# Five outer products instead of three in a 4x2x3 block scheme, early first addends out of PSUM, and one-level Strassen for two side products

## The chip, the cores and the metric

The kernel runs on one core of a Trainium2 chip. The metric is the device time of one execution in microseconds (us): the median of repeated runs, lower is better. The core has a matrix engine (PE, with weight loads shown apart as PEld), three engines for elementwise work (DVE, the vector engine; ACT, the scalar engine; POOL, GpSimd), and queues that issue transfers (SP's and ACT's hardware queues, and POOL's own, which can add to the destination while it moves). PE writes only to PSUM, eight banks of 512 float32 per partition; everything else lives in SBUF, 128 partitions wide.

## The reference

For x of 1024 x 512, a weight of 64 x 512 x 512 (embedding e, feature f, model column m), and a linear layer of 512 x 512, all float32:

```python
out_lin = x @ lin_w.T + lin_b
xv = jnp.einsum('bf,efm->bem', x, weight)
zp = jnp.einsum('bf,efm->bem', jnp.square(x), jnp.square(weight))
interaction = 0.5 * jnp.sum(jnp.square(xv) - zp, axis=1)
return out_lin + interaction
```

The large part is `xv`: a product of 1024 x 512 with 512 x 32768, of which only the sum of squares over e is kept. The sum over e of `zp` is one product of 1024 x 512 with 512 x 512, once the squares of the weight are summed over e. `out_lin` is another product of that size.

## The kernel before, in words

**Groups.** The 512 columns m are cut into 22 groups (`GROUPS`): two of 16 columns, then twenty of 24. A group is 64 times as many columns of the large product: 1024 for the first two, 1536 for the others. The host has laid the weight out so that a group is four quadrants (feature half by column half), each of 2 x 768 elements per partition (`iw` = 768; 512 in the first two groups).

**Outer level.** Each group is one 2 x 2 by 2 x 2 block product by the Strassen-Winograd scheme: seven outer products, numbered 1 to 7 and run in `ORDER` 1, 6, 5, 2, 7, 4, 3. Their left operands X1 to X7 are made once at the start from x. Their right operands (`RHS`) are weight quadrants or sums of quadrants, which POOL's adding transfers make in place (`outer_sum`). The scheme's running sums over outer products are kept in four SBUF tiles `oa` to `od`: `TARGET` names the tile that an outer product writes and `ADDEND` the one that it adds to its own result. After outer products 7 and 4, `outer_out` adds `od` to `ob` and to `oc`, two adding transfers each.

**Inner level.** An outer product is 512 x 256 by 256 x 768, and there are two ways to do it. `tree` (L630) is again 2 x 2 x 2 Strassen-Winograd: seven products of two matmuls, 384 columns each (256 in the first two groups), so 14 matmuls. `wide_tree` (L719) is a 4 x 2 x 3 scheme: 20 matmuls of 256 columns. A float32 matmul shows in the trace as two PE instructions. Before, `HK` = (1, 5, 7) are wide in the groups of 24 and the other four are narrow; in the two groups of 16 all seven are narrow. A wide left operand needs 20 blocks in place of 14; `widen` (L542) makes them once, after the group of 16 that used X last. The right-hand sums of a product (in tile `t`) are POOL's: three instructions for a narrow one (768, 384, 384 elements), seven for a wide one (768, 512, 512 and four of 256).

**Leaving PSUM.** Four pairs of banks are shared: `b1`, `b3` ("fresh") and the ring `b2_0`, `b2_1`. A wide outer product uses three pairs: two banks T, U of a fresh pair, Q and S of one b2 pair, R and V of the other. Running sums inside PSUM are started by copies from bank to bank on ACT (`copy`) and go on by accumulating matmuls. `leave` takes a finished bank out to the target: a copy on ACT where nothing is added, else an addition on DVE. Values that are needed twice are parked by ACT in the small tiles `p5` and `p53` (rings of two buffers): `pp`, `p19` and `n5` of a wide product, `p5` of a narrow one. Where such a parked value and an `ADDEND` must both be added and the product is not in `EARLY`, POOL adds one of them (both are in SBUF) and DVE the other. Where it is in `EARLY` (before: 2 alone), DVE adds the bank to the addend at once, straight out of PSUM, and adds again later; nothing is parked and POOL does nothing.

**After a sum is complete** (outer products 2, 5, 4, 3), `finish` squares it on ACT and reduces it over e on DVE into `acc`: 16 pairs of instructions of 768 elements a group. `w_squares` does the same with the weight quadrants into `w2_sum`, eight pairs a group.

**First and last stage.** At the start, 32 matmuls of 512 columns (L503) make `out_lin`; it goes to DRAM. At the end, 32 matmuls of 512 columns (L950) multiply -0.5 x squared by `w2_sum`; DVE adds the saved `out_lin` and half of `acc`, and the result leaves.

**Order.** All instructions are put into a list (`Plan`), with costs per engine, and `Plan.order` (L175) plays that list against its cost model: each engine takes its next ready operation by latest start, PE by `key`. The result is a fixed program order for each engine. `AHEAD_OF` (L37) is a table of small shifts of the due times, one per operation kind. The costs stand in `tt`, `copy`, `square`, `reduce`, `dma`, `dma_add` (L413 to L458). PE may take an operation up to `AHEAD` = 20 us before its turn. On the chip each engine executes its list strictly in that order.

Of the kernel before, what the change touches and what calls it, by code (L numbers as in the profile page):

```python
# [12 lines left out]
AF = mybir.ActivationFunctionType  # L13
# [6 lines left out]
HK = (1, 5, 7)  # L20
EARLY = (2,)
# [14 lines left out]
SPARE = -99.0  # L36
AHEAD_OF = """  # L37
0:l 1:hvhc 2:3bp 3:hvw0 4:37v 5:338 6:3g7 7:34e 8:1o 9:33e a:33f b:-d c:369 d:-2 e:28 f:1 g:-1v h:-k i:-2k
j:-o k:-5 l:-26 m:8 n:7 o:i p:2a q:d r:15 s:b t:29 u:q v:-5 w:4 x:-k z:m 10:-9 11:d 12:-5 13:g 14:w 15:-2
16:10 17:-b 18:-e 19:17 1a:f 1b:1b 1c:l 1d:-14 1e:-c 1f:-3 1g:-11 1h:m 1i:7 1j:2 1k:8 1l:6 1m:-g 1n:-2 1o:-r  # L40
1p:-h 1q:m 1r:-r 1s:a 1t:5 1u:j 1v:-f 1w:3 1x:a 1y:o 1z:-g 20:3 21:-p 22:-g 23:g 24:2tw 25:2xs 26:f 28:38f
29:314 2a:-8 2b:-26 2c:9 2d:-4 2e:-8 2f:i 2g:-l 2h:-2 2i:d 2j:z 2k:-a 2l:13 2m:l 2n:m 2o:-7d 2p:-7 2q:-1 2r:1h
2s:-h 2t:-u 2u:ao 2v:-d 2w:-c 2x:-k 2y:7 2z:d 30:13 31:s 32:1u 33:-m 34:-j 35:-14 36:-i 37:-c 38:4 39:c 3a:18
3b:b 3c:-5 3d:l 3e:8 3f:1 3g:23u 3h:k 3i:1m 3j:g 3k:d 3l:1w1 3m:f 3n:-18 3o:-c 3p:5 3q:-i 3r:-g 3s:o 3t:-2
3u:-17 3v:3 3w:-q 3x:-t 3y:m 3z:m 40:-4 41:1rk 42:-a 43:-f 44:2 45:5 46:-1b 47:-1r 48:-4j 49:-s 4a:-t 4b:-3
4c:-o 4d:1d 4e:b 4f:2 4g:-r 4h:j 4i:-i 4j:1s 4k:-4 4l:4 4m:f 4n:3 4o:-7 4p:-l 4q:1j 4r:-b 4s:a 4t:c 4u:-2 4v:2
4w:m 4x:-1a 4y:-1 4z:-5 50:2 51:-2 52:-5 53:-5 54:r 55:x 56:13 57:n 58:20 59:1vi 5a:f 5b:-2 5c:1q 5d:-d 5e:1u1
5f:8 5g:-f 5h:3 5i:-2 5j:7 5k:36 5l:17 5m:-h 5n:-7 5o:10 5p:15 5q:i 5r:-w 5s:g 5t:f 5u:c 5v:-s 5w:1 5x:j 5y:6
5z:4d 60:e 61:13 62:d 63:-p 64:k 65:-b 66:17 67:-g 68:-k 69:-m 6a:1g 6b:x 6c:a 6d:-5 6e:5 6f:-7 6g:1e 6h:-4
6i:z 6j:-h 6k:-3h 6l:-22 6m:n 6n:-1n 6o:r 6p:y 6q:a 6r:10 6t:m 6u:-9 6v:-2 6w:2n 6x:-18 6y:-1h 6z:1 70:m  # L50
71:-1e 72:-k 73:-4 74:-3 75:-d 76:9 78:-o 79:-3 7a:-t 7b:-k 7c:-7 7d:-s 7e:b 7f:-9 7g:-1i 7h:-13 7i:19 7j:j
7k:1h 7l:-24 7m:c 7n:-2 7o:5 7p:-3 7q:q 7r:r 7s:q 7t:b 7u:1a 7v:v 7w:q 7x:-4 7y:-1p 7z:10 80:19 81:-o 82:m
83:c 84:-u 85:1 86:-1 87:-2 88:-4 89:-4 8a:-5 8b:-11 8c:3 8d:c 8e:-r 8f:x 8g:-w 8h:-u 8i:-5 8j:-1p 8k:-3
8l:-1e 8m:y 8n:o 8o:1f 8p:-1 8q:5 8r:-2 8s:1xv 8t:j 8u:7 8v:-7 8w:-f 8x:-u 8y:f 8z:1 90:e 91:6 92:-h 93:18
94:r 95:n 97:-1a 98:-c 99:-p 9a:-e 9b:8 9d:-11 9e:-3 9f:e 9g:-n 9h:-a 9j:-16 9k:-f 9l:-2 9m:h 9n:3 9o:f 9p:-5
9q:-2b 9r:v 9s:-18 9t:o 9u:o 9v:232 9w:8 9x:c 9y:-n 9z:d a0:-7 a1:-a a2:5 a3:-h a4:u a5:i a6:-d2 a7:8 a8:-n
a9:8 aa:-do ab:1a ac:i ad:-12 ae:11 af:2 ag:s ah:-n ai:-9 aj:-9 ak:3 al:l am:-fj an:-5 ao:2sx ap:d aq:13 ar:-4
as:2 at:t au:-9 av:-y aw:-l ax:-2 ay:9 az:v b0:-3 b1:-8 b2:l b3:-13 b4:g b5:-b b6:-1g b7:7 b8:-15 b9:-1 ba:-f
bc:-o bd:-b be:j bf:e bg:s bh:-1i bi:-1q bj:-1g bk:n bl:g bm:4 bn:a bo:-g bp:g bq:1 br:8 bs:-c bt:-1r bu:1e
bv:-1p bw:z bx:d by:m bz:-1f c0:-p c1:-5 c2:2 c3:q c4:-1j c5:-8 c6:j c7:e c8:-f c9:-b ca:5 cb:f cc:-k cd:1c  # L60
ce:-1n cf:-3 cg:-5 ch:-s ci:-m cj:-9 ck:-k cl:-7 cm:r cn:-a co:a cp:-n cq:-q cr:-10 cs:-w ct:b cu:-a cv:-10
cw:1g cx:-12 cy:j cz:-v d0:-14 d1:1b d2:-g d3:-g d4:8 d5:8 d6:-16 d7:n d8:j d9:-r da:-4 db:-13 dc:1d dd:-15
de:-9 df:16 dg:19 dh:d di:a dj:z dk:-a dl:-9 dm:-1w dn:-w do:-4 dp:p dq:b dr:-1w ds:2x dt:-b du:-e dv:-4 dw:3
dx:-t dy:g dz:8 e0:d e1:-5 e2:-g e3:-u e4:w e5:-r e6:j e7:4 e8:o e9:e ea:9 eb:a ec:-f ed:-16 ee:-l ef:k eg:-d
eh:-1g ei:i ej:-4 ek:-o el:-u em:5 en:-1f eo:-4 ep:5 er:7 es:s et:-1p eu:-9 ev:-b ew:o ex:i ey:-j ez:c f0:-14
f1:-u f2:-11 f3:5 f4:-l f5:c f6:-q f7:5 f8:k f9:-1 fa:-1e fb:1 fc:-1f fe:-j ff:-1 fg:5 fh:t fi:-q fj:-g fk:-8
fl:4 fm:-1o fn:10 fo:b fp:-3 fq:-13 fr:r fs:2 ft:-19 fu:1b fv:-t fw:-5 fx:-14 fy:-5 fz:-k g0:-6 g1:-6 g2:-2
g3:-1w g4:1o g6:-e g7:a g8:q g9:-d ga:-5 gb:8 gc:-h gd:9 ge:-5 gf:-7 gg:a gh:6 gi:-h gj:2 gk:-11 gl:-6 gm:4
gn:e go:1v gp:-14 gq:s gr:6 gs:-v gt:3 gu:3 gv:d gw:-6 gx:1q gy:-2 gz:-19 h0:-1m h1:-1h h2:-h h3:-5 h4:-g
h5:-14 h6:-2 h7:z h8:-j h9:f ha:-b hb:-6 hc:10 hd:-14 he:9 hf:e hg:-6 hh:-n hi:-a hj:y hk:-2 hl:-8 hn:6 ho:-t  # L70
hp:-g hq:-2 hr:-14 hs:c ht:4 hu:1 hv:a hw:-15 hx:-l hy:i hz:-d i0:-8 i1:-8 i2:-8 i3:11 i4:-7 i5:-13 i6:1h i7:b
i8:2 i9:7 ia:-8 ib:a ic:6 id:-m ie:2 if:4 ig:6 ih:-o ii:-a ij:-8 ik:n il:c im:u in:x io:-6 ip:a iq:-g ir:s
is:g it:l iu:-m iv:-1l iw:-2 ix:16 iy:-1o iz:-q j0:-y j1:-a j2:u j3:q j4:z j5:-1t j6:3 j8:-h j9:-c ja:12
# [947 lines left out]
```

## Time and profile before

| | |
|---|---|
| median of 3 runs | 1416.3 us (1412.21 to 1417.54) |
| the profiled execution | 1415.96 us |
| its span, first to last instruction | 1414.2 us |
| DVE busy | 1100.0 us (78%) x1461 |
| ACT busy | 806.0 us (57%) x1293 |
| POOL busy | 1173.7 us (83%) x1117 |
| granted PE clock, mean | 0.997 of full speed |

In the rows below, a line of a group of instructions gives the line of the code, the engine, output and inputs, the shape and the count, then the busy time in us and the mean duration in ns, then the idle time before them and what ended it. A line of the chain of waits gives its start in us, its length, and what ran. A line of the timeline gives start, length, engine, line, operation and, in brackets, the idle time before it and what released it. A line of the windows gives a stretch and, for each engine, its busy time with the number of instructions, then the PE clock, the share of the transfer engines and GB/s.

### The profile page before, as it was taken

The numbers are of one execution on the slowest core, as the hardware profiler recorded it, in microseconds if no ns is written. First come the engines' busy times: TensorE is split into PE (matmuls) and PEld (weight loads), VectorE is DVE, ScalarE is ACT, GpSimd is POOL, SyncE is SP. The second block draws the span as 40 slices with busy tenths as digits, with TensorE's granted clock in tenths as the row PEclk, the third lists the DMA queues.
The fourth block names the chain that finished last, engine by engine and source line by source line (L and its number), as shares of the span: only waits on it lengthen the run. The fifth ranks groups of instructions, "written<-read, shape, count | busy, mean of one in ns | idle before, by whom it ended". The sixth has DMA issues, their size and how long they took to land.

```text
span 1414.2 us, 16647 instructions
## 1 busy us (share of the span) xinstructions
PE 1396.6 (99%) x5160; PEld 971.5 (69%) x5160; DVE 1100.0 (78%) x1461; ACT 806.0 (57%) x1293; POOL 1173.7 (83%) x1117
## 2 busy tenths in 40 slices
PE   8999989999999999999999999999999999999998
PEld 3887757767776766767676676777677677767663
DVE  2678678878878786887879688787968878796895
ACT  1456465656757465665656566565746556574642
POOL 5999978897979798797979879897987989788870
PEclk9999999999999999999999999999999999999999
DMA  8589596777949676795968678596958859694773
GB/s 260 164 192 227 135 202 153 165 188 161 228 120 228 160 178 171 167 223 117 230 159 192 160 180 208 131 222 146 216 143 195 197 132 221 135 238 109 163 193 112
DMA packets 92599, 251.76 MB, mean 178 GB/s; under 512 B 29472, under 2 KB 30496, under 8 KB 92512
## 3 DMA queue, kind: packets, MB, share of 16 engines
q0 software_dynamic: 26448, 134.49, 49.6%
q1 hardware_dynamic: 65488, 115.17, 24.0%
q8 instruction: 42, 0.69, 0.2%
q10 hardware_dynamic: 576, 1.05, 0.2%
q14 instruction: 45, 0.37, 0.1%
HBM read 127.04 MB, written 6.19 MB: 94 GB/s over the span
## 4 chain that ended last, share of the span: by engine, by line
PE 90%; POOL 4%; DMA 4%; DVE 1%; issue 1%; ACT 0%; SPq 0%; POOLq 0%; DVEq 0%; ACTq 0%
PE b L464 51%; PE b_r L464 18%; PE b_l L464 17%; POOL t L421 2%; PE b_r L950 1%; PE b_l L950 1%; DMA oc<-od 1%; DMA T<-T1a 1%; DMA oa<-xT 1%; PE b_l L503 1%; PE b_r L503 1%; DMA w<-weight 1%; POOL X L421 1%; DMA X<-xT 0%; POOL ob L456 0%
## 5 line engine op out<-in xcount | busy, mean ns | idle before, releaser
L464 PE MATMUL b<-t,X 128*128 128x384 f32 (+1 forms) x1504 | 518.5, 474 | 1.9 <-DVE ob L421 1.1
L464 PEld LDWEIGHTS b<-t,X 128*128 128x128 f32 x1504 | 276.1, 190 | 168.4 <-DVE oa L421 18.8
L421 POOL TENSOR_TENSOR t<-t,w 128x256 f32<-128x256 f32 (+1 forms) x200 | 232.6, 1287 | 9.0 <-PE b L464 5.7
L421 POOL TENSOR_TENSOR t<-w 128x768 f32<-128x768 f32 (+1 forms) x88 | 163.0, 1860 | 88.1 <-PE b_l L464 70.5
L438 ACT ACTIVATE oa<-oa 128x768 f32<-128x768 f32 (+1 forms) x176 | 142.8, 822 | 134.5 <-DVE oa L421 132.4
L464 PE MATMUL b<-w,X 128*128 128x384 f32 (+1 forms) x576 | 193.9, 469 | 0.1
L464 PE MATMUL b_l<-t,X 128*128 128x256 f32 x720 | 189.6, 381 | 3.9 <-ACT b_l L431 3.9
L464 PE MATMUL b_r<-t,X 128*128 128x256 f32 x600 | 167.9, 383 | 0.4 <-DVE ob L421 0.3
L447 DVE TENSOR_REDUCE acc<-oa 128x12 f32<-128x768 f32 (+1 forms) x176 | 161.6, 920 | 3.7 <-ACT oa L438 3.7
L447 DVE TENSOR_REDUCE w_sum<-wsq 128x12 f32<-128x768 f32 (+1 forms) x176 | 161.5, 920 | 1.1 <-ACT wsq L438 1.0
L464 PEld LDWEIGHTS b_l<-t,X 128*128 128x128 f32 x720 | 137.2, 191 | 32.2 <-ACT b_l L431 4.5
L464 PEld LDWEIGHTS b<-w,X 128*128 128x128 f32 x576 | 109.1, 190 | 56.5 <-ACT p L431 2.1
L464 PEld LDWEIGHTS b_r<-t,X 128*128 128x128 f32 x600 | 113.9, 191 | 47.7 <-issue 5.0
L438 ACT ACTIVATE wsq<-w 128x768 f32<-128x768 f32 (+1 forms) x132 | 107.3, 821 | 38.8 <-DVE w_sum L447 16.9
L421 DVE TENSOR_TENSOR oa<-b,oa 128x768 f32<-128x768 f32 (+1 forms) x88 | 82.0, 932 | 59.6 <-PE b L464 55.7
L421 POOL TENSOR_TENSOR t<-w,t 128x384 f32<-128x384 f32 (+1 forms) x96 | 107.7, 1122 | 2.4
L431 ACT COPY b<-b 128x768 f32<-128x768 f32 (+1 forms) x94 | 71.2, 757 | 60.3 <-PE b L464 58.0
L464 PE MATMUL b_r<-w,X 128*128 128x256 f32 x400 | 99.8, 380 | 0.0
L464 PE MATMUL b<-T,X 128*128 128x384 f32 (+1 forms) x264 | 91.3, 477 | 0.6 <-DMA T<-T1a 0.6
L421 DVE TENSOR_TENSOR oa<-b,oc 128x768 f32<-128x768 f32 (+1 forms) x66 | 61.2, 930 | 34.7 <-PE b L464 32.9
L464 PEld LDWEIGHTS b_r<-w,X 128*128 128x128 f32 x400 | 76.3, 191 | 14.3
L421 POOL TENSOR_TENSOR oc<-ob,p 128x512 f32<-128x512 f32 (+1 forms) x80 | 82.3, 1105 | 3.6 <-ACT p L431 2.0
(143 smaller groups left out, 2618.1 us busy)
## 6 DMA issues: line engine op xcount, KB each, us to landing
w<-weight SPq DMA_DIRECT2D x120, 384.0 KB, 6.0
ob<-od POOLq DMA_DIRECT2D x40, 768.0 KB, 7.9
oc<-od POOLq DMA_DIRECT2D x40, 768.0 KB, 9.5
T<-weight SPq DMA_DIRECT2D x40, 384.0 KB, 4.0
w<-T POOLq DMA_DIRECT2D x20, 768.0 KB, 6.5
T1a<-weight SPq DMA_DIRECT2D x20, 384.0 KB, 3.3
w22a<-weight SPq DMA_DIRECT2D x20, 384.0 KB, 8.8
T1a<-weight POOLq DMA_DIRECT2D x10, 768.0 KB, 11.9
```

Source lines behind the costliest of these rows:

```text
L421: return f(o.ap, a.ap, b.ap)
L431: return nc.scalar.copy(o.ap, i.ap)
L438: lambda _: nc.scalar.activation(o.ap, i.ap, AF.Square), i.atoms, o.atoms)
L447: nc.vector.tensor_reduce(o, x, axis=AX.X, op=ALU.add)
L464: nc.tensor.matmul(a.ap, b.ap, w.ap, start=start, stop=True, skip_group_check=True)
L503: nc.tensor.matmul(o[j].ap, x.ap[:, ts((g * 2 + j) % (NB // 2), P)], w.ap, start=(k == 0), stop=(k == NK - 1),)
L950: nc.tensor.matmul(z.ap, view(xe[h, k // KH])[:, k % KH, ts((g * 2 + j) % (NB // 2), P)], reg("w2_sum", k * M, M).ap, start=(k == 0), stop ...
```

## The change

It makes outer products 6 and 2 wide as well (five wide, two narrow in the groups of 24), puts 3, 4, 6, 7 beside 2 into `EARLY`, cuts the two parking rings to one buffer each, and does `out_lin` and the product of the squares by one level of Strassen-Winograd (seven products `big` of eight 256-column matmuls, 56 in all). PE gets four matmuls on zeros at the start (`WARM`). At the end the squares of x are made on ACT, and the whole result is assembled by quadrants. The planner's costs for ACT's and the transfers' operations and the table `AHEAD_OF` are new, so the fixed orders of all engines are new too.

```diff
-HK = (1, 5, 7)
-EARLY = (2,)
+HK = (1, 5, 6, 2, 7)
+EARLY = (2, 3, 4, 6, 7)
...
+HALF = 0.5 ** 0.5
+WARM = 4
+P5S = 1
+P53S = 1
...
-    p5_ring = ring([make(f"p5_{k}", WIDE) for k in range(2)])
+    p5_ring = ring([make(f"p5_{k}", WIDE) for k in range(P5S)])
...
-        plan.add({ACT: 0.19 + 0.00083 * o.size}, emit, i.atoms, o.atoms,
+        plan.add({ACT: 0.06 + 0.00083 * o.size}, emit, i.atoms, o.atoms,
...
-    def dma(o, i, reads, writes, cost=2.4, land=1.5, queue=nc.sync):
-        plan.add({SP: cost}, lambda _: queue.dma_start(o, i), reads, writes, land=land)
+    def dma(o, i, reads, writes, moves=1.3, land=1.8, queue=nc.sync):
+        plan.add({SP: 0.4}, lambda _: queue.dma_start(o, i), reads, writes, land=land, queue=moves)
...
-        plan.add({POOL: 1.0}, emit, reads + writes, writes, land=2.0, queue=3.1 * rows / 1024)
+        plan.add({POOL: 0.7}, emit, reads + writes, writes, land=1.8, queue=2.5 * rows / 1024)
...
+    C = M // 2
+    lw_in(0, 0, nc.scalar)
+    x_load(0, 0, nc.sync, 2)
+    lw_in(1, 0, nc.scalar)
+    x_load(0, 1, nc.sync)
+    lw_in(0, 1, nc.scalar)
+    lw_in(1, 1, nc.scalar)
+    x_load(1, 1, nc.sync)
+    x_load(1, 0, nc.sync)
...
+    plan.add({DVE: 0.8}, lambda _: nc.vector.memset(zero.ap, 0.0), (), zero.atoms)
+    for n in range(WARM):
...
+    tt(two(lsum[1]), lw(0, 1, (M, KH)), lw(0, 0, (M, KH)), only=DVE)
+    tt(two(lsum[2]), lw(1, 1, (M, KH)), two(lsum[1]), only=DVE)
+    tt(two(lsum[4]), lw(1, 0, (M, KH)), two(lsum[2]), only=DVE)
+    tt(two(lsum[7]), lw(0, 1, (M, KH)), lw(1, 1, (M, KH)), only=DVE)
...
-    tt(x_block(5), x_in(1, 1), x_in(1, 0), True)
+    tt(x_block(5), x_in(1, 1), x_in(1, 0), True, DVE)
     minus_both(x_block(6), x_block(5), x_in(0, 0))
-    tt(x_block(7), x_in(0, 0), x_in(1, 0), True)
+    tt(x_block(7), x_in(0, 0), x_in(1, 0), True, DVE)
...
+    def outer_products(xs, ws, base_key, ready, leave):
+
+        u2, u3, m4, m5 = "b2_0", "b1", "b3", "b2_1"
+        big("b1", xs[1], ws[1], True, base_key)
+        copy(pair(u2), pair("b1"))
+        big("b1", xs[2], ws[2], False, base_key + 1)
+        leave(0, 0, "b1")
+        big(m4, xs[4], ws[4], True, base_key + 2)
+        ready(0, m4)
+        big(m5, xs[5], ws[5], True, base_key + 3)
+        ready(1, m5)
+        big(u2, xs[6], ws[6], False, base_key + 4)
+        copy(pair(u3), pair(u2))
+        big(u3, xs[7], ws[7], False, base_key + 5)
+        leave(1, 0, u3)
+        leave(1, 1, u3)
+        big(u2, xs[3], ws[3], False, base_key + 6, ((0, 0, 2), (1, 0, 2), (0, 2, 4), (1, 2, 4)))
+        leave(0, 1, u2)
...
-    for (h, q), x in xe.items():
-        dma(view(x), x_src[:, ts(q, KH), ts(h, H)], (), x.atoms)
-        plan.add(
-            {DVE: 1.24},
...
+    for (h, q), x in x2.items():
+        dma(x.ap.rearrange("p (a m) -> p a m", a=KH), x_src[:, ts(q, KH), ts(h, H)], (), x.atoms)
+        plan.add({ACT: 0.10 + 0.00083 * x.size},
+                 lambda _, x=x: nc.scalar.activation(x.ap, x.ap, AF.Square, scale=HALF),
+                 x.atoms, x.atoms)
...
+    def leave(h, c, b):
+        r = rest[h, c]
+        n = 1 if (h, c) != (0, 1) else 2
+        for k in range(n):
+            o = Reg(r.tile, r.off + k * 2 * N // n, 2 * N // n)
+            tt(o, o, reg(b, k * 2 * N // n, 2 * N // n), c == 0)
+            dma(out_dst[:, 4 * h + k * 4 // n:4 * h + (k + 1) * 4 // n, ts(c, C)],
+                o.ap.rearrange("p (a m) -> p a m", m=C), o.atoms, ())
+
+    outer_products(xs, ws, 1e6, ready, leave)
```

More of the change, by code (lines that the diff above doesn't have):

```diff
@@ new lines, in pair @@
+    def pair(name):
+        return reg(name, 0, 2 * N)
+    zero = reg("t", 0, P + N)
+    plan.add({DVE: 0.8}, lambda _: nc.vector.memset(zero.ap, 0.0), (), zero.atoms)
+    for n in range(WARM):
+        z, o = reg("t", 0, P), bank(f"b2_{n // 2}", n % 2)
+        zw = reg("t", P, N)
+        plan.add({PE: 1.8 * mm_cost(N)},
+                 lambda _, z=z, o=o, zw=zw: nc.tensor.matmul(o.ap, z.ap, zw.ap, start=True, stop=True),
+                 zero.atoms, o.atoms, key=-2000 + n, banks=o.banks(True))
@@ L519, in x_block, with lw_sum @@
+    def lw_sum(i):
+        return lambda k: Reg(lsum[i].tile, lsum[i].off + k * C, C)
     def x_block(i):
@@ new lines @@
+    other = last + 1
+    rooms = []
+    for name in (w(other, "w22"), w(other, "T1"), "w11", "X1", "X6", w(last, "T1"), "X5", "X2",
+                 "w12", "X7", "T2", "w21", "X4"):
+        rooms += [reg(name, k * 2 * N, 2 * N) for k in range(buf[name].size // (2 * N))]
+    spare = [w(other, "w22"), w(other, "T1"), "w11", w(last, "T1")]
+    spare = iter([reg(n, 2 * N, N) for n in spare])
+    rooms = iter(rooms)
+    x2 = {(h, q): next(rooms) for h, q in ((0, 0), (0, 1), (1, 1), (1, 0))}
```

390 lines of the change are left out of this document (220 added, 170 removed).

## The prediction

> **What bounds the kernel now.** First the page: how busy PE is, and whose work lies on the chain that ended last.
>
> ```profile
> PE 1396.6 (99%) x5160; PEld 971.5 (69%) x5160; DVE 1100.0 (78%) x1461; ACT 806.0 (57%) x1293; POOL 1173.7 (83%) x1117
> ...
> PE 90%; POOL 4%; DMA 4%; DVE 1%; issue 1%; ACT 0%; SPq 0%; POOLq 0%; DVEq 0%; ACTq 0%
> ```
>
> PE is busy without a break, and nine tenths of the chain is PE. A busy PE need not be at its pace, so next comes the chain in the middle of the run, for the pace and the period.
>
> ```profile
> 608.46 1.73 PE b_l L464 x8
> ...
> 614.50 15.51 PE b L464 x48
> ...
> 739.29 15.51 PE b L464 x48
> ```
>
> The pattern comes back after 739.29 - 614.50 = 124.79 us, two groups: **62.40 us a group**. A matmul is two instructions. At 384 columns one takes 15.51 / 24 = 0.646 us, at 256 columns 1.73 / 4 = 0.4325 us. A group has 4 x 14 = 56 of the first and 3 x 20 = 60 of the second: 36.2 + 25.95 = 62.1 us. So waits cost 0.3 us a group, and only PE work can be won there. Then the windows, for the other engines in a steady group, at a bad place and at the end.
>
> ```profile
> 177.60:240.00 62.40, 58.49 (x213) 41.42 (x212) 46.25 (x62) 34.23 (x56) 46.71 (x45) 0.95 0.73 164
> ...
> 302.40:364.80 62.40, 62.40 (x234) 43.46 (x233) 50.15 (x67) 37.57 (x61) 52.38 (x50) 1.00 0.79 184
> ...
> 155.00:177.60 22.60, 22.46 (x83) 15.30 (x82) 15.47 (x22) 10.89 (x17) 22.30 (x24) 1.00 0.71 180
> ...
> 1360.00:1381.00 21.00, 20.80 (x71) 13.11 (x71) 19.58 (x22) 7.94 (x12) 15.14 (x12) 1.00 0.90 219
> ```
>
> The columns are PE, PEld, DVE, ACT, POOL. In the steady group DVE has 12.2 us free and POOL 10.0. Before 178 us POOL is full; near the end DVE is. One stretch lost PE time and clock; the timeline shows why.
>
> ```profile
> 191.34 0.84 ACT L438 ACTIVATE wsq<-w 128x768 f32<-128x768 f32 x1 [5.35 <-DMA w<-weight]
> 192.09 0.58 ACT L431 COPY b_l<-b_r 128x512 f32<-128x512 f32 x1
> 192.72 1.22 PE L464 MATMUL b_l<-t,X 128*128 128x256 f32 x2 [3.91 <-ACT b_l L431]
> ...
> 198.00 1.25 PE L464 MATMUL b_l<-w,X 128*128 128x256 f32 x5
> ```
>
> A square at the head of ACT's list waited for a late weight load; the copy behind it was what PE needed. PE stood 3.91 us, and then its next 12 instructions took 198.00 - 192.72 = 5.28 us in place of 12 x 0.216 = 2.6: together 6.6 us, once.
>
> **PE's part of the change.** Products 6 and 2 go from 14 matmuls of 384 to 20 of 256: per product 14 x 0.646 = 9.04 us becomes 20 x 0.4325 = 8.65. Two per group: the need falls from 62.1 to 28 x 0.646 + 100 x 0.4325 = 61.3, **0.8 us a group, 16 us over twenty groups**. The groups of 16 columns stay narrow.
>
> **What the other engines must now do per group.** POOL first, by its groups of instructions.
>
> ```profile
> L421 POOL TENSOR_TENSOR t<-w 128x768 f32<-128x768 f32 x80 | 152.1, 1908 | 88.0 <-PE b_l L464 70.5 <-DMA w<-T 10.2 <-issue 4.7
> L421 POOL TENSOR_TENSOR t<-t,w 128x512 f32<-128x512 f32 x80 | 126.2, 1578 | 8.2 <-PE b L464 5.7
> L421 POOL TENSOR_TENSOR t<-t,w 128x256 f32<-128x256 f32 x120 | 106.4, 1094 | 0.8
> L421 POOL TENSOR_TENSOR t<-w,t 128x384 f32<-128x384 f32 x80 | 93.4, 1168 | 2.2
> L421 POOL TENSOR_TENSOR oc<-ob,p 128x512 f32<-128x512 f32 x40 | 56.1, 1410 | 0.8
> L421 POOL TENSOR_TENSOR oa<-oa,oc 128x768 f32<-128x768 f32 x20 | 47.5, 2375 | 0.1
> L421 POOL TENSOR_TENSOR ob<-p,ob 128x768 f32<-128x768 f32 x20 | 39.3, 1966 | 2.9 <-DVE p L421 2.9
> L421 POOL TENSOR_TENSOR ob<-ob,oa 128x768 f32<-128x768 f32 x20 | 36.6, 1828 | 4.5 <-ACT b_l L431 4.5
> L421 POOL TENSOR_TENSOR oc<-ob,p 128x256 f32<-128x256 f32 x40 | 32.0, 801 | 2.8 <-ACT p L431 2.0
> L421 POOL TENSOR_TENSOR X<-X 128x256 f32<-128x256 f32 x43 | 37.0, 884 | 13.6 <-ACT X L431 8.4 <-DVE X L527 4.6
> L421 POOL TENSOR_TENSOR X<-X 128x128 f32<-128x128 f32 x21 | 12.6, 701 | 0.0
> ```
>
> Right-hand sums: a narrow product needs 1.9 + 2 x 1.17 = 4.2 us, a wide one 1.9 + 2 x 1.58 + 4 x 1.09 = 9.4. Two more wide ones add 10.4. `EARLY` takes away POOL's additions for 4, 3, 6 and 7: (47.5 + 39.3 + 36.6 + 56.1 + 32.0) / 20 = 10.6. POOL stays at 52 of 61 us. I cost this at nothing: the sums run a product ahead of PE, under its matmuls; without that cover each wide product would begin some 2 us late, on its first sum.
>
> ACT exchanges five copies of 768 elements, one of 512 and one of 256 for eight of 512 and two of 256: 4608 elements both ways, in three more instructions. Its 37.57 us become 38 to 39, nothing on the path.
>
> DVE is where the work goes. Here are its durations and its spacing when work is queued.
>
> ```profile
> L421 DVE TENSOR_TENSOR oa<-b,oa 128x768 f32<-128x768 f32 x80 | 76.5, 956 | 51.8 <-PE b L464 50.8
> L447 DVE TENSOR_REDUCE acc<-oc 128x12 f32<-128x768 f32 x80 | 73.8, 943 | 0.0
> L421 DVE TENSOR_TENSOR oa<-b_l,p 128x512 f32<-128x512 f32 x40 | 25.9, 686 | 3.6 <-PE b_l L464 2.9
> ...
> 648.61 1.80 DVE L447 TENSOR_REDUCE acc<-oc 128x12 f32<-128x768 f32 x2
> ...
> 672.19 1.29 DVE L421 TENSOR_TENSOR oc<-oc,b_l 128x512 f32<-128x512 f32 x2
> ...
> 674.68 0.42 DVE L421 TENSOR_TENSOR oc<-oc,b_r 128x256 f32<-128x256 f32 x1 [0.51 <-ACT p L431]
> 675.02 0.41 DVE L421 TENSOR_TENSOR oc<-ob,b_r 128x256 f32<-128x256 f32 x1
> ```
>
> Queued instructions overlap: 768 elements every 1.80 - 0.94 = 0.86 us, 512 every 1.29 - 0.69 = 0.60, 256 every 0.34. From the code a group before has 24 reductions and 21 additions of 768, 8 of 512, 13 of 256: 45 x 0.86 + 8 x 0.60 + 13 x 0.34 = 47.9 us, and the window shows 50.15 busy. An early wide product has 5 of 512 and 10 of 256, 6.4 us; it replaces 4.3 (narrow 6), 5.2 (narrow 2) and 4.1 (wide 7). Early 4 and 3 have one more of 768 each. After: 36 of 768, 19 of 512, 38 of 256 = **55.3 us of 61.3, 90%**. With full durations (0.95, 0.69, 0.42) it would be 63.4, more than PE needs; with the busy share of before (50.15 of 53.8) 59.1. I take 55 to 59: DVE fits, with little room.
>
> What that costs PE: a narrow early product must have its first bank added out by DVE (0.96) before the product after next writes that bank (1.29 us later), so a DVE in the middle of a reduction holds PE. Two such products a group, up to 0.6 each; none, if the order keeps DVE free there. I take waits of 0.8 us a group in place of 0.3: period 61.3 + 0.8 = 62.1 would win 0.3, and without any growth 61.6 wins 0.8. The wide products, whose banks are reused only three products (1.3 us) or more after each copy, make me go between, **61.85: 0.55 x 20 = 11 us** won. Bounds: 63.4 (a loss of 20 us) to 61.3 (a win of 22).
>
> The single parking buffer: `p19` of a wide product is last read after its 16th matmul and written again after the next one's 4th, 8 x 0.43 = 3.5 us later. Nothing, unless DVE is over 3 us late.
>
> **Sums ahead of time.** `ob` now gets its first addend out of PSUM at product 3's first bank, not its fourth: 3 x 1.29 = 3.9 us earlier. It waits for the second adding transfer.
>
> ```profile
> 679.62 1.17 POOL L456 DMA_DIRECT2D ob<-od  x1
> ...
> 689.11 0.95 DVE L421 TENSOR_TENSOR ob<-b,ob 128x768 f32<-128x768 f32 x1
> ...
> DMA to landing us min/median/max: 6.6/8.4/9.5
> ```
>
> It lands at 679.62 + 8.4 = 688.0; the first reader moves from 689.1 to 685.2. It can be issued when product 7 has read `ob`, which now ends with DVE at about 676: 676 + 1 + 8.4 = 685.4. Even, within 1 us. If it is late, DVE's list stands behind that addition, reductions and other banks' additions with it, and PE for the banks; PE has products 1 and 6 to put in between. Cost 0 in the forecast, up to 1 us a group as a bound.
>
> **The start.** Lines of the timeline, the last two of the chain of waits:
>
> ```profile
> 5.50 2.05 PE L503 MATMUL b_l<-ob,oa 128*128 128x512 f32 x2 [5.50 <-DMA oa<-xT]
> ...
> 9.31 1.04 ACT L431 COPY X<-oa 128x1024 f32<-128x1024 f32 x1
> ...
> 10.52 1.02 PE L503 MATMUL b_r<-ob,oa 128*128 128x512 f32 x2
> ...
> 35.73 1.03 PE L464 MATMUL b<-t,X 128*128 128x256 f32 x4
> ...
> 1381.32 3.43 PE b_l L950 x8
> ...
> 1410.11 0.69 DVE X L421
> ```
>
> `out_lin` took 35.73 - 5.50 = 30.2 us for 64 instructions that need 64 x 0.429 = 27.5; the first ones ran at half pace. After: 56 x 0.4325 = 24.2 us. The zeros, 8 instructions, can start near 1.7 us, once DVE has written them; if six are slow and take 5 us, as 5.50 to 10.52 shows, and two take 0.43 each, they end about 7.6 with the data there; one bank copy (1024 elements, 1.0 us and two hand-overs, 1.3) has nothing beside it. 7.6 + 24.2 + 1.3 = 33.1: **2.5 us** won. Bounds: 0 (both copies and a late sum of x open) to 6 (data at 5.5, nothing open).
>
> The Trainium skill ("TensorE: Matmul & The Clock Gate", Part 1: The HAM clock gate) says that PE starts at half clock and gets the full one after about 3.4 us of activity, and loses it after an idle window of that length. The slow instructions at 5.5 us and after the 3.91 us wait agree; the zeros take that cost off the real work, by this rule as by the rows.
>
> Two more `widen` are some 5 x 0.88 + 7 x 0.7 = 9.3 us of POOL each, 18.6. Against that, `EARLY` saves six additions of 512 (two thirds of 2.06 us each, the mean of the three rows of 768: 8.2), and two sums of 1024 go to DVE (2.5 each, from the row of 768). That is 5 us more where POOL is full, due in the third group, where the 6.6 us were lost. The new order may keep that wait out, as its costs now put loads and adding transfers into one queue. I take half: **3 us** won; bounds -5 to 6.6.
>
> The Trainium skill ("GPSIMD Engine Reference", 1. Specifications) says that POOL shares SBUF interfaces with DVE and contends with DVE instructions that have two SBUF inputs. Here that speaks against the sums of x and of the linear weight that go to DVE (some 5 us of DVE by its spacing), and for `EARLY`; no row here separates it. By it the start would win 0 rather than 3.
>
> **The end.** PE needs 28.8 us from 1381.32 to its last instruction; 24.2 + 1.3 for one bank copy makes 25.5, less 2 to 3 us. But DVE is full there (19.58 of 21), gets 7.4 us more in the last group, less the squares of x that go to ACT, and now PE waits for its additions: banks are used twice. I take **1.5**; bounds -4 to 3.
>
> **The sum.** 11 + 2.5 + 3 + 1.5 = 18 us off the profiled execution's 1415.96, with the 1.8 us outside its span unchanged: **1398**. The median of the runs, 1416.3, stands 0.3 above that execution, too little to correct for.
>
> **Rivals.**
> 1. *DVE becomes the bound.* For: 90% by spacing, 63.4 by durations. Against: its idle time before was mostly waiting for PE. It decides once DVE's need passes 61.9 us a group. At 63.2 the twenty groups lose 0.8 x 20 = 16, the start and the end win 4 to 5: **1427**. Chance 0.09.
> 2. *Waits eat the gain.* The early reader of `ob` and the narrow early banks each hold PE 0.3 us more, period 62.3: 2 us won in the groups, 2.5 at the start: **1411**. For: transfers of up to 9.5 us. Chance 0.14.
> 3. *Everything fits.* Period 61.45, the one stall gone: 19 + 6.6 + 2.5 + 1.5 = 29.6 off, **1386**. For: PE waited only 0.3 us a group before. Chance 0.20.
>
> The forecast (1392 to 1408) has 0.57. A change under 0.5% (7 us) can't be told from none here: faster 0.77 (forecast and 3), same 0.14 (2), slower 0.09 (1). The range 1386 to 1413 leaves out 1 and half of 3, some 19 in 100.
>
> **What would show it.** The period between equal patterns in the chain: 61.6 to 62.1 if right. DVE's busy time in a steady group: 57 to 60. POOL near 50. Trees starting near 33 us, and near 190 us PE waits of half the 3.91 us or less. A period over 62.4 with PE waiting for DVE's `oa`, `ob` or `oc` lines would make the prediction wrong by rival 1; waits ended by `ob<-od`, by rival 2.

## The result, and where the time went

The changed kernel takes **1456.9 us** (median of 4 runs, 1450.5 to 1459.1) against 1416.3 for the kernel before (1412.2 to 1417.5): a ratio of 1.028, 95% interval 1.025 to 1.032. It is slower, where 1398 and a win of 18 us were forecast, and outside the range of 1386 to 1413. The profiled execution took 1455.98 us, with a span of 1454.2.

The page of the changed kernel: busy time by engine, and the shares of the chain that ended last.

```profile
PE 1410.9 (97%) x5744; PEld 1069.0 (74%) x5744; DVE 1252.9 (86%) x2012; ACT 808.1 (56%) x1355; POOL 1124.9 (77%) x1137
...
PE 64%; DMA 15%; DVE 8%; ACT 5%; issue 4%; POOL 4%; ACTq 0%; DVEq 0%; POOLq 0%
```

PE was 90% of the chain and is 64%: in a third of the time the chain now runs through other work. The tree of product 3 starts with a matmul of the tile w22a in every even group, so its line in the timeline is a mark for measuring. Here it is in groups 4 and 20 (counted from 0), and PE's last matmuls, first of the kernel before:

```profile
308.58 0.49 PE L464 MATMUL b<-w22a,X 128*128 128x384 f32 x1
...
1307.28 0.49 PE L464 MATMUL b<-w22a,X 128*128 128x384 f32 x1
...
1408.19 1.88 PE L950 MATMUL b_r<-w_sum,X 128*128 128x512 f32 x4
```

and of the changed kernel:

```profile
323.62 0.49 PE L487 MATMUL b<-w22a,X 128*128 128x384 f32 x1
...
1344.08 0.49 PE L487 MATMUL b<-w22a,X 128*128 128x384 f32 x1
...
1448.98 1.13 PE L544 MATMUL b<-w_sum,X 128*128 128x256 f32 x4 [0.78 <-DVE X L444]
```

The sixteen groups between the marks took 998.70 / 16 = 62.42 us each before and 1020.46 / 16 = **63.78 us** after. The 40.0 us between the ends of the last matmuls (1410.07 and 1450.11) split at the marks: 15.0 up to group 4, 21.8 in the sixteen groups, 3.2 behind group 20. The prediction had all three falling.

The load on the engines came out as forecast. The windows of the changed kernel (PE, PEld, DVE, ACT, POOL, then the granted clock, the DMA share and GB/s):

```profile
120.00:240.00 120.00, 107.25 (x436) 81.58 (x435) 92.72 (x156) 63.75 (x116) 94.48 (x102) 0.96 0.65 154
...
302.40:364.80 62.40, 61.50 (x250) 46.20 (x249) 55.08 (x91) 36.81 (x63) 47.57 (x47) 1.00 0.76 179
```

In the steady stretch of 62.4 us DVE is busy 55 us, ACT 37, POOL 48. PE lost the time in waits. Adding up, over the trace, by how much each matmul instruction starts later than 0.216 us (256 columns), 0.323 (384) or 0.429 (512) behind the one before it gives 87 us lost in the changed kernel and 24 before. The need of PE by these spacings fell by 19 us (22.5 less the 3.4 for the matmuls on zeros), its first instruction starts 3.9 us earlier, and the losses grew by 63: together the 40 us. (The expectations below put the two losses at 86 and 27.)

**One wait, taken apart.** The timeline of the changed kernel in product 6, PE, ACT and DVE:

```profile
664.96 0.57 ACT L454 COPY b_l<-b_l 128x512 f32<-128x512 f32 x1
665.07 0.41 DVE L444 TENSOR_TENSOR ob<-oa,b_r 128x256 f32<-128x256 f32 x1
665.52 0.37 ACT L454 COPY p<-b_r 128x256 f32<-128x256 f32 x1
665.59 0.70 PE L487 MATMUL b_l<-T,X 128*128 128x256 f32 x2
665.92 0.42 DVE L444 TENSOR_TENSOR ob<-oa,b_r 128x256 f32<-128x256 f32 x1 [0.44 <-ACT p L454]
666.40 0.70 PE L487 MATMUL b_r<-T,X 128*128 128x256 f32 x2
666.93 1.46 PE L487 MATMUL b_l<-T,X 128*128 128x256 f32 x6
```

Both DVE instructions are first addends: `ob` gets `oa` plus a sum that stands in the right half of a bank. ACT's copy parks the same sum as `p19`. None of the three needs another's result, all only read the bank; yet the second addition stands idle for 0.44 us and starts 0.03 after the copy ends (665.89). DVE's line names the copy as what ended its wait. (The copy itself starts 0.04 us after the first addition, but ACT was busy with the copy before it until then, so that start proves nothing.) PE's next write to that bank (product 14) was due at 666.12, 0.53 us after the pair at 665.59, which had waited too, and starts at 666.40, 0.06 after the second addition. The two instructions then take 0.53 us to the next line, not 0.43: this wait cost PE 0.10 more behind it. So, in this program, reads of one PSUM bank by ACT and by DVE are taken in turn, by semaphore. No line of kernel.py asks for it: its function `follow` ties reads of a bank to writes alone, so these semaphores come in when the program is built. No run leaves them out. The Trainium skill ("PSUM — Partial Sum Buffer", PSUM bank collisions raise a hardware error) says that two engines must be kept apart on a bank by a semaphore, reads against reads included; the trace agrees, with 0.03 to 0.04 us from one read to the next. The prediction passed that rule by.

The same turn-taking was there before the change, and at the place shown it cost PE nothing. The kernel before, product 5:

```profile
344.46 1.45 PE L464 MATMUL b<-t,X 128*128 128x384 f32 x4
...
345.10 0.37 ACT L431 COPY p<-b_r 128x256 f32<-128x256 f32 x1 [0.49 <-DVE od L421]
...
346.18 0.59 PE L464 MATMUL b_r<-t,X 128*128 128x256 f32 x2
```

and the same place after:

```profile
678.76 1.03 PE L487 MATMUL b_l<-t,X 128*128 128x256 f32 x4
...
679.62 1.34 PE L487 MATMUL b_r<-t,X 128*128 128x256 f32 x4
...
679.83 0.37 ACT L454 COPY p<-b_r 128x256 f32<-128x256 f32 x1 [0.49 <-DVE od L444]
```

The copy waits 0.49 us for DVE in both. Before, matmuls of a narrow product stood between the wide one's (the 384-column line), and PE came to the bank at 346.18, 0.7 us after the copy. After, products 1, 6, 5, 2 and 7 are all wide and follow each other, PE comes at once, and four instructions take 1.34 us in place of 1.03. Such waits between 300 and 1200 us are not much longer than before: 90 to 100 instructions of ACT and DVE waited 41 to 44 us for the other's read before, 100 to 120 waited 48 to 50 us after, by how one counts. What changed is above all that PE stands behind them. In the views of waits (us in total, times, longest) the first line is of the kernel before, the other two of the changed one:

```profile
PEld b L464 <- DVE oa L421: 20.4, 60, 1.2
...
PEld b L487 <- DVE oa L444: 22.8, 53, 2.2
PEld b_r L487 <- ACT p L454: 19.0, 37, 1.2
```

PE's weight loads wait for DVE's additions into `oa` about as before; their waits for the parked copies (`p`) at the wide products' banks are new. Added up over all such lines, those behind additions into `oa`, `ob` and `oc` grew from 32 to 50 us and those behind ACT from 9 to 47.

**The other cause** is DMA. From the page of the kernel before, KB and median us to landing:

```profile
ob<-od POOLq DMA_DIRECT2D x40, 768.0 KB, 7.9
oc<-od POOLq DMA_DIRECT2D x40, 768.0 KB, 9.5
...
w22a<-weight SPq DMA_DIRECT2D x20, 384.0 KB, 8.8
```

and of the changed kernel:

```profile
ob<-od POOLq DMA_DIRECT2D x40, 768.0 KB, 9.5
oc<-od POOLq DMA_DIRECT2D x40, 768.0 KB, 14.6
T<-weight SPq DMA_DIRECT2D x40, 384.0 KB, 3.6
...
w22a<-weight SPq DMA_DIRECT2D x20, 384.0 KB, 11.8
```

The adding transfers land later, and a load beside them takes three times as long as one alone (11.8 against 3.6 us: between 130 and 1300 us an adding transfer was under way beside every load of `w22a`, and beside 5 of 36 loads of `T`). Where the transfers of `outer_out` are left out (run no_outer_out, below), the same load needs 4.4 us:

```profile
w22a<-weight SPq DMA_DIRECT2D x20, 384.0 KB, 4.4
```

How late transfers reach PE, in the timeline of ACT and PE of the changed kernel:

```profile
661.80 0.84 ACT L461 ACTIVATE oc<-oc 128x768 f32<-128x768 f32 x1 [1.26 <-DMA oc<-od]
662.55 0.37 ACT L453 ACTIVATE oa<-b_r 128x256 f32<-128x256 f32 x1
662.82 0.59 ACT L454 COPY b_r<-b_l 128x512 f32<-128x512 f32 x1
663.33 0.38 ACT L454 COPY p<-b_r 128x256 f32<-128x256 f32 x1
...
663.76 1.99 PE L487 MATMUL b_r<-t,X 128*128 128x256 f32 x8 [0.72 <-ACT p L454]
```

A square at the head of ACT's list waits for `oc<-od`; the copies behind it are what PE needs. The one-off stall of the prediction is the same thing, larger:

```profile
187.98 0.84 ACT L461 ACTIVATE wsq<-w 128x768 f32<-128x768 f32 x1 [8.56 <-DMA w<-weight]
...
195.56 0.79 ACT L454 COPY b<-b 128x768 f32<-128x768 f32 x1
...
196.50 2.90 PE L487 MATMUL b<-t,X 128*128 128x384 f32 x4 [8.26 <-ACT b L454]
```

PE stands 8.26 us (3.91 before) and then runs at half pace: four instructions of 384 columns take 2.69 us to the next, not 1.29.

### The profile page after: what moved, and what is told of

The parts are those of the page before. It is cut to its first block, busy times and chain, and to the rows that moved or that the text cites. A ratio compares the mean times of both kernels' runs of the same rounds, so it can differ in the third digit from the quotient of the medians.

```text
span 1454.2 us, 18499 instructions
## 1 busy us (share of the span) xinstructions
PE 1410.9 (97%) x5744; PEld 1069.0 (74%) x5744; DVE 1252.9 (86%) x2012; ACT 808.1 (56%) x1355; POOL 1124.9 (77%) x1137
## 4 chain that ended last, share of the span: by engine, by line
PE 64%; DMA 15%; DVE 8%; ACT 5%; issue 4%; POOL 4%; ACTq 0%; DVEq 0%; POOLq 0%
PE b_r L487 24%; PE b_l L487 20%; PE b L487 17%; DMA oc<-od 6%; DMA ob<-od 5%; POOL t L444 2%; PE b L544 2%; DVE ob L444 2%; DVE oa L444 2%; DMA w<-weight 2%; DMA w<-T 2%; ACT oc L461 1%; DVE acc L470 1%; ACT p L454 1%; DVE w_sum L470 1%
## 5 line engine op out<-in xcount | busy, mean ns | idle before, releaser
L444 POOL TENSOR_TENSOR t<-t,w 128x512 f32<-128x512 f32 x300 | 316.6, 1112 | 76.7 <-PE b L487 67.0
L487 PE MATMUL b<-t,X 128*128 128x384 f32 (+1 forms) x864 | 287.7, 465 | 16.4 <-ACT b L454 10.2
L487 PE MATMUL b_l<-t,X 128*128 128x256 f32 x1200 | 303.3, 380 | 0.0
L487 PE MATMUL b_r<-t,X 128*128 128x256 f32 x1000 | 277.2, 387 | 8.8 <-ACT p L454 3.7
L487 PEld LDWEIGHTS b_l<-t,X 128*128 128x128 f32 x1200 | 226.8, 190 | 35.5 <-DVE ob L444 1.9
L487 PEld LDWEIGHTS b<-t,X 128*128 128x128 f32 x864 | 160.2, 191 | 110.1 <-POOL t L444 15.2
L461 ACT ACTIVATE wsq<-w 128x768 f32<-128x768 f32 (+1 forms) x132 | 107.6, 822 | 53.1 <-DMA w<-weight 37.5
L487 PE MATMUL b_l<-w,X 128*128 128x256 f32 x480 | 115.4, 379 | 0.0
L487 PE MATMUL b<-w,X 128*128 128x384 f32 (+1 forms) x336 | 110.3, 458 | 1.8 <-DMA w<-T 1.5
L444 POOL TENSOR_TENSOR t<-t,T 128x256 f32<-128x256 f32 (+1 forms) x100 | 96.5, 968 | 12.7 <-PE b_l L487 7.0
L487 PEld LDWEIGHTS b_l<-w,X 128*128 128x128 f32 x480 | 90.9, 190 | 12.9 <-ACT b_l L454 0.5
## 6 DMA issues: line engine op xcount, KB each, us to landing
oc<-od POOLq DMA_DIRECT2D x40, 768.0 KB, 14.6
w22a<-weight SPq DMA_DIRECT2D x20, 384.0 KB, 11.8
```

Source lines behind the costliest of these rows:

```text
L444: return f(o.ap, a.ap, b.ap)
L461: lambda _: nc.scalar.activation(o.ap, i.ap, AF.Square), i.atoms, o.atoms)
L487: nc.tensor.matmul(a.ap, b.ap, w.ap, start=start, stop=True, skip_group_check=True)
```

## The experiments

The theories. **D**: DVE's load (rival 1). **H**: hand-overs between engines last longer than the planner counts. **B**: shared banks, as above. **T**: late transfers. The edits keep the planner's list of each engine unless they say so. The runs that leave something out were run once each, and the changed kernel's own four runs lie 8.6 us apart, so a few us of difference in time say little; the period is the better measure, though each kernel has one trace and how far its period varies was not measured. The mark of group 4 holds the one stall near 190 us, which is 8.26 us in the changed kernel's trace, 9.2 in half_reduce, 9.4 in first_sbuf, 5.7 in half_squares, 3.1 in parked_sbuf and under 1 in act_first: several us of that column go with it, whatever was edited. The marks are the ones used above.

| run | time, us | mark of group 4 | us a group | behind group 20 |
|---|---|---|---|---|
| before | 1416.3 | 308.6 | 62.42 | 102.8 |
| changed | 1456.9 | 323.6 | 63.78 | 106.0 |
| half_reduce | 1449.2 | 322.2 | 63.51 | 104.9 |
| half_squares | 1444.7 | 318.9 | 63.38 | 105.8 |
| no_outer_out | 1427.9 | 307.7 | 63.18 | 103.5 |
| act_first | 1463.9 | 317.4 | 64.62 | 106.8 |
| parked_sbuf | 1445.3 | 317.1 | 63.11 | 112.6 |
| first_sbuf | 1444.5 | 319.8 | 63.34 | 105.5 |
| all_three | 1409.2 | 304.6 | 61.95 | 107.6 |
| after_retuned | 1429.6 | 311.6 | 62.57 | 110.4 |
| after_slack | 1424.7 | 312.3 | 62.39 | 107.6 |
| before_retuned | 1417.8 | 305.6 | 62.57 | 106.1 |
| before_slack | 1415.7 | 306.1 | 62.49 | 105.3 |
| three_wide_slack | 1430.6 | 315.9 | 63.19 | 100.9 |
| squares_only | 1412.5 | 307.3 | 62.04 | 108.8 |

**half_reduce: less work for DVE.**

```diff
                 x = x.rearrange("p (m e) -> p m e", e=E)
+            x = x[:, :, :E // 2] if len(x.shape) == 3 else x[:, :, :, :E // 2]
```

> The changed kernel in its own order of instructions, with every reduction of products with e reading only the first 32 of the 64 values it sums (so acc is computed from half of them). Nothing moves on any engine; only DVE's 24 reductions a group become shorter, by about 0.4 us each, some 10 us of DVE a group. If DVE's load is what PE waits for (theory D: 55 of 63 us a group, banks and parked copies come free late behind the queue of reductions), PE's lost time in a steady group falls from 2-3 us to under 0.7 and the period between equal patterns to 61.8 or less, the time to 1415-1425. If it is the hand-overs from ACT and DVE to PE's weight loads, each some 0.1 us longer than the order leaves room for (theory H), the reductions only stand beside them: period 62.8 or more, time 1440 or more. In between: the two share it.

1449.2 us and 63.51 us a group, with DVE's busy time in a steady window down from 55.1 to 48.4 us. D asked for 61.8 or less; 0.27 us a group is what came back. D falls as the main cause.

**half_squares: less work for ACT.**

```diff
-        square(r, r)
+        square(r, r, True)     # reads and writes only the first half of each tile's columns
```

> The changed kernel in its own order, with the squares that are made for the second half of the output on ACT covering only the first half of each tile's columns. ACT has some 6 us a group less to do, nothing moves. If ACT's copies come late because they stand in its queue behind squares, the period falls by 0.5 us a group or more and the time to 1445 or less. By theory D (DVE's load) and by theory H (length of a hand-over, not a queue) the period stays within 0.3 of the 63.2-63.9 measured, the time at 1448-1458.

1444.7 us and 63.38, 0.40 a group: the time is what "ACT's queue" asked for, the period lies between its 0.5 and the 0.3 of the others, and 4.7 us are in the mark of group 4, of which the smaller stall is 2.6. ACT's list may matter where copies stand behind squares; the main cause it is not.

**no_outer_out: no adding transfers into memory.**

```diff
             dma_add(x.ap, y.ap, 2 * iw, y.atoms, x.atoms)
+            plan.ops[-1].emit = None
```

> The changed kernel in its own order, without the adding transfers that write the outer sums to memory (the output lacks the sums of the main loop). The tiles oa, ob and oc are then free at once for their next writers. Theory T (transfers that land late hold DVE's first addition into ob and oc and, through the shared queue, the weight loads): the waits of DVE on ob<-od go, the period falls by 0.5-1 us, the stall near 190 us (about 8 us of PE waiting and 3 us at half clock) is gone; time 1425-1440. By theories D and H only the stall near 190 us can go (at most 12 us), the period stays at 63 or more: 1443-1457.

1427.9 us. The stall near 190 us is gone, and the mark of group 4 comes 15.9 us earlier, ahead of the kernel before: most of the early loss is T's. The period falls by 0.60, and 63.18 is still 0.76 above before, so T is not the whole of the steady loss.

At this point the traces showed the turn-taking described above, waits that no dependence in the plan explains. From here on B is tested, with the help of a **replay**: the five lists, each in order, with durations, spacings and hand-overs taken from the two traces, the turn-taking, and transfers fitted to their landing times. It is a calculation, and no run shows its terms by themselves (among them 0.2 us for a matmul that waited, where the pair above shows 0.10).

**act_first: the same lists, woven together otherwise.**

```diff
-    for op, engine in plan.order():
+    for op, engine in act_first(plan.order()):
+    # act_first: the five lists merged by planned start, ACT's counted 1 us earlier
```

> The changed kernel with the same list of instructions in the same order on every engine; only the order in which the lists are woven together when they are issued to the program is another: an ACT instruction is put ahead of other engines' instructions that the plan starts up to 1 us earlier. Nothing is left out. Theory B (a read of a PSUM bank by ACT and one by DVE of the same bank are kept apart by a semaphore, in the order of issue, though neither needs the other's result): the waits change sides, DVE's additions out of PSUM now stand behind ACT's copies of the same bank, and as DVE is the fuller engine the time changes by several us; in-order replay of the lists with the durations measured in the changed kernel's trace says 12 us more, so 1462-1475. Theory D (DVE's load) and theory H (length of a hand-over) see the same lists and the same true dependences and expect the time within 4 us of the changed kernel's 1457.

1463.9 us, and a period of 64.62: 0.84 us a group more with not an instruction moved on any engine. D has no way to see that; B had it within its range. (The early part came out 6 us better, so the sum is +7.) And the waits did change sides. The first line is of the changed kernel's view of waits, the second of this run's:

```profile
ACT p L454 <- DVE od L444: 9.3, 19, 0.5
...
DVE od L444 <- ACT p L454: 15.7, 20, 2.5
```

These are the same places in both, product 5's copy into `p` and the addition into `od` that reads the same bank, in 19 groups. Whichever is issued first goes first and the other waits. H could see a change only if hand-overs had grown longer; for ACT's copies behind PE they are the same (0.04 us where the copy waits for one semaphore, 0.09 in the median for two, in both traces).

**parked_sbuf: the parked copies leave the banks.**

```diff
-        copy(p19, h("U", 1))
+        copy(p19, h("U", 1), instead=reg(f"X{i}", 0, V))
...
-            copy(n5, h("S", 1))
+            copy(n5, h("S", 1), instead=reg(f"X{i}", 0, V))
```

> The changed kernel in its own order, with ACT's 140 copies of 256 columns into the parking buffers (p19 and n5 of the wide products) reading a tile of SBUF in place of the PSUM bank, so that these sums are wrong; ACT's time is the same. PE no longer waits for these copies and no copy shares a bank with a DVE addition. Theory B: the period falls from 63.2-63.9 to about 62.7-63.0, the time by some 15 us to 1438-1446, as these copies carry 19 of the 50 us that ACT and DVE wait for each other's reads between 300 and 1200 us. Theory D: the period stays (DVE does what it did), 1450 or more. Theory H: the two hand-overs to PE per wide product that went give back at most 0.1 us each, 5 products x 0.1 x 20 = up to 10 us, 1447 or more.

1445.3 us, B's time, at 63.11 a group, a little over B's 62.7 to 63.0; ACT and DVE do as much as ever. By the time alone H's 1447 or more is not ruled out, one run against another. Behind group 20 it loses 6.6 us, which stays unexplained.

**first_sbuf: the first addends leave the banks.**

```diff
-                tt(f(o, *at), f(a, *at), h(b, half), sub)
+                tt(f(o, *at), f(a, *at), h(b, half), sub, instead=f(a, *at))
```

> The changed kernel in its own order, with the first addends of the wide products 6, 2 and 7 (DVE's additions that now read a PSUM bank ahead of time) taken from SBUF alone: the addend is copied by a DVE instruction of the same number of elements and the bank is not read, so that these sums lack a term. DVE's list and load stay; these instructions neither wait for ACT's reads of the bank nor hold ACT's reads or PE's next write. Theory B with the first addends as its main carrier: period 62.9-63.3, time 1436-1446 (replay: 14 us less). If the missing narrow products between the wide ones are the whole matter (the parked copies and not the first addends), 1450 or more.

1444.5 us, in B's range, at 63.34, just over B's 62.9 to 63.3: the first addends are worth about 12 us in all, as much as the parked copies that they share banks with, and 0.44 a group against their 0.67.

**all_three: these two and no_outer_out together.**

> The changed kernel in its own order with three edits together: the copies into the parking buffers read SBUF, the first addends of the wide products read SBUF, and the adding transfers that write the outer sums are left out (the output is wrong in all these sums; the matmuls, squares, reductions and loads are all there). If shared banks (B) and late transfers (T) are the two causes of the 40 us, the period is 62.2 or less and the time 1400-1412, below the kernel before. If a third cause holds PE in the main loop: period over 62.6, time 1418 or more.

1409.2 us. The marks of this run:

```profile
304.56 0.49 PE L494 MATMUL b<-w22a,X 128*128 128x384 f32 x1
...
1295.74 0.49 PE L494 MATMUL b<-w22a,X 128*128 128x384 f32 x1
```

991.18 / 16 = **61.95 us a group**, and its steady window:

```profile
302.40:364.80 62.40, 62.40 (x259) 48.13 (x258) 57.10 (x94) 37.95 (x64) 45.91 (x46) 1.00 0.54 132
```

With the banks unshared at these two places and the transfers away, PE is busy throughout while DVE does 57 us of the window. That is the period that the prediction gave (61.85), at the load that it gave. Steady state: B and T are the causes, 1.83 us a group together (0.67, 0.44 and 0.60 one by one). Away from the edited places hand-overs are left as they were in this run, and so are the single parking buffers, which the change cut from two; neither can be a main cause of the 1.36 us that the change lost a group. (The edits also take away waits that the kernel before had, so they win more than the change lost. And they take whole reads off the banks: what the turns cost apart from the reads themselves is not shown.)

**after_retuned and before_retuned: another order, nothing else.** Only the numbers in `AHEAD_OF` differ; they were chosen by the replay.

```diff
 AHEAD_OF = """
-0:-9 1:lck 2:all 3:ls0 4:lgs ...
+(another table)
 """
```

> The changed kernel with another table AHEAD_OF and nothing else: the same instructions, costs and planner, in an order that was searched for by replaying each candidate's five lists with what the traces show (a read of a bank waits for the other engine's read of it; a matmul that waits costs 0.2 us more; an adding transfer 3.8 us of the queue, a load beside it moving at a fifth of its pace). Order theory (B and T: the same work, badly placed for waits that its planner does not know): losses fall from 86 us to 22, the time to 1388-1405, faster than before. Theory D (90% load on DVE holds PE in any order): 1435 or more.

> The kernel before with another table AHEAD_OF, searched for in the same way, and nothing else. Its need of PE is 1390 us; the replay finds an order that loses 2 us in place of the 27 measured. Expected 1392-1404: then an order made for the waits of the chip is worth some 15-20 us to either kernel, and the change is to be judged against this one. If the replay is wrong about the chip: 1412 or more.

1429.6 us (ratio to before 1.009, 1.007 to 1.012) and 1417.8 (1.002, 1.000 to 1.003). Order gives back 27 of the 40 us, with DVE's load untouched: D falls again. But both runs miss what was expected by the replay, 1388-1405 and 1392-1404, by 25 and 14 us; as a forecast the replay was wrong. A likely reason, not tested by itself: a search finds the orders at whose margins the model is wrong, and the trace has longer hand-overs than the minimum (last section).

**after_slack and before_slack: orders made with longer hand-overs.** Again only the table.

> The changed kernel with a third table AHEAD_OF and nothing else, searched for as in the first such run, but counting every hand-over 0.015 to 0.05 us longer than its minimum and adding transfers up to 4.0 us, so that the order keeps some slack. By the replay 1388 to 1411. If order is the whole matter (B and T), 1400-1418, level with the kernel before or a little faster, and the period 62.2 or less; if the first such order (1429.6) was already as good as five wide products allow, 1425 or more.

> The kernel before with a table AHEAD_OF found by the same search with the same slack, and nothing else. By the replay 1400 to 1407 plus 2 outside the span; its need of PE alone is 1390. Expected 1403-1414; the difference to the changed kernel with such an order is what the change itself is worth with orders of equal making.

1424.7 us (1.007, 1.005 to 1.010) and 1415.7 (1.0005, 0.999 to 1.002). The changed kernel misses its 1400-1418 and lies at the edge of the other answer, 1425 or more; before_slack comes out above its 1403-1414. The changed kernel's period is 62.39, level with before. So the loss in the main loop belongs to five wide products in the order that the change came with: with an order that knows the banks they win nothing there and lose nothing. What is left, 8 to 9 us against the kernel before, is ahead of group 4 and behind group 20.

**three_wide_slack: the Strassen level at both ends alone.**

```diff
-HK = (1, 5, 6, 2, 7)
-EARLY = (2, 3, 4, 6, 7)
+HK = (1, 5, 7)
+EARLY = (2,)
...
-P5S = 1
-P53S = 1
+P5S = 2
+P53S = 2
```

> One part of the change alone: lin and the squares by one Strassen level, and the planner's new costs, with the kernel before's three wide products (HK 1, 5, 7), first addends (EARLY 2) and two of each parking buffer; the table AHEAD_OF is searched for with the same slack, and the plan counts a read of a bank as waiting for the other engine's read of it. Need of PE: 5 us less than before. By the replay 1400-1410. If the loss sits in the five wide products and the first addends, the period is that of before, 62.4-62.6, and the time 1403-1416; if the Strassen level at the two ends costs what it saves, 1416 or more.

1430.6 us (1.011, 1.008 to 1.014), a miss: the period is 63.19 though its products are those of before, so this order is worse by 0.8 us a group, and its mark of group 4, at 315.9, comes 7 us late. A poor order costs as much with three wide products as the banks cost with five, so this run does not place the loss in the five. Only the end says something: 100.9, 1.9 under before. (Its plan also counts the turns at a bank, in the function that says when an operation is ready.)

**squares_only: the kernel before with the Strassen level for the squares alone**, in an order of its own. The edit puts the changed kernel's code behind `plan.mark("end")` in place of the old one.

> The kernel before with one part of the change alone: the matmuls of the squares at the end by one Strassen level (56 instructions of 512 columns' worth in place of 64, the additions on DVE between), lin at the start, the three wide products and the first addends as before; the table AHEAD_OF is searched for with the same slack as for the two kernels above. Its need of PE is 3.4 us less than before. If the end of the changed kernel (40.9 us from its last group's pattern against 38.0 before) is long only because the last group's DVE work is in its way, the end here falls to some 35 us and the time to 1406-1413, below both kernels. If the Strassen level at the end costs what it saves (additions of 1024 on DVE and single buffers behind the last matmuls), the end stays at 38 or more and the time at 1413-1420.

1412.5 us, ratio 0.9984 (0.9972 to 0.9996): a little below the kernel before, by less than 0.3%, and the fastest kernel here that computes everything. But not for the reason expected: its end is longer (108.8), and its gain is an order with a period of 62.04.

## Why the prediction was wrong

- **PE's need: right.** 61.3 us a group was forecast; all_three runs at 61.95 with some waits left, and over the whole trace the need fell by 22.5 us without the zeros.
- **The load of DVE, ACT and POOL: right.** 55 to 59 of DVE was forecast, 55.1 to 57.1 measured; ACT 37 against 38 to 39; POOL 48 against "near 50". DVE at 90% did not hold PE: all_three has it at the same load.
- **"What that costs PE": the step that failed.** It took waits of 0.55 us a group, from DVE's queue and the two narrow banks, and let the wide products go free because "banks are reused only three products (1.3 us) or more after each copy". Measured: 63.78 - 61.3 = 2.5 us a group. A bank is not free after one copy when ACT and DVE both read it: three reads in turn, 0.41, 0.37 and 0.42 us with hand-overs between, fill those 1.3 us. act_first shows the turns, and parked_sbuf and first_sbuf what such reads cost: about 1.1 of the 2.5. The step also missed that narrow products stood between the wide ones; that they hid the turns is read from the one place shown above, and no run tests it alone.
- **"Sums ahead of time", cost 0 and up to 1 us a group: wrong.** The transfers `ob<-od` and `oc<-od` do not land "even": their medians rose to 9.5 and 14.6 us, and they hold loads up. no_outer_out puts this at 0.6 us a group and up to 16 us before group 4.
- **The one-off stall, half of it won: wrong in sign.** PE's wait went from 3.91 to 8.26 us. The planner's new costs do put loads and adding transfers into one queue; in the trace they share it unevenly, and the square at 187.98 stood 8.56 us for its load (5.35 before).
- **The start, 2.5 us won, and the end, 1.5: both lost.** The first matmul of `w22a` in group 0 starts at 73.58 us against 71.47 before, 2.1 us late. The zeros did what they were for: the first matmuls of `out_lin`, at 6.56, run at full pace, 16 instructions in 3.62 us. But PE waits 1.56 us for the bank copy at 11.74 (1.3 was forecast) and 1.75 for a sum of POOL at 37.72. Behind group 20 the changed kernel takes 3.2 us more. three_wide_slack gains 1.9 there and squares_only loses 6.0, with the same Strassen code, so the order around it seems to decide; which part of it stays open.
- **The rivals.** Rival 2 named waits behind early readers and `ob<-od`, the right kind, with 0.6 us a group where 2.5 were lost, and at the narrow products, not the wide ones. Rival 1, the only slow one, was not what happened, though its sign came: a period over 62.4, with PE waiting longer for DVE's additions (the 32 and 50 us above). half_reduce takes 7 us of 55 off DVE's work and leaves those waits at 44 us; DVE was late at the banks, not full. What was missing was a rival for the rule on banks. The view of waits of the kernel before already held the line:

```profile
ACT p L431 <- DVE od L421: 9.3, 19, 0.5
```

19 waits of a copy for an addition out of PSUM (9.3 us in total, at most 0.5), with no data passing between them. The question "why does ACT wait for DVE here?" leads to the turns at a bank.

## What to carry to other kernels

Before work is moved onto another engine's read of PSUM, list for each bank who reads it between two writes of PE, and add those reads up in a row: here reads by two engines did not overlap, and the row must fit between PE's visits. When a filler (here narrow products between wide ones) is replaced by work that PE does faster, ask what stood in its shadow. An order is tuned to its cost model: put a wait that the trace shows into the model before tuning, and trust a tuned order only after a run; four such orders here came out 2 to 25 us slower than the slow end of what was expected of them.

## What the hardware showed that was not expected

- Reads of one bank by ACT and DVE, kept in turn by the program's semaphores, 0.03 to 0.04 us from the end of one to the start of the next.
- Often a matmul that waited is followed by a gap: in the changed kernel's trace, of 228 pairs of 256 columns behind a wait of 0.1 to 1.5 us, some 120 took 0.51 to 0.54 us in place of 0.43, and 103 took 0.43.
- A hand-over goes with how many semaphores the instruction waits for: of ACT's instructions that PE released in the changed kernel's trace, all 44 with one semaphore started 0.04 us after the matmul's end; of 126 with two, 95 needed 0.09 to 0.10; with three, 46 needed 0.08 in the median.
- Loads starve beside adding transfers: 384 KB took 3.6 us in the median where hardly any ran (T<-weight), 11.8 beside them (w22a<-weight), and 4.4 for the same load without those of `outer_out`.
